# A message-passing layer: the tail's first one-hots stand two steps later in the written order

## The chip, the core and the metric

The kernel runs on one core of a Trainium2 chip. Its engines work side by side, each through its own list of instructions in order: PE multiplies matrices (its weight loads show as PEld), DVE and ACT work on vectors, POOL issues the scatters, SP issues most transfers. The time is device microseconds of one execution. Before the change three runs took 1111.35, 1112.56 and 1113.34 us; the median is 1112.56.

## What is computed

A graph layer with 6250 nodes, 100000 edges and 128 features:

```python
msg_in = jnp.concatenate([x[row], x[col], edge_attr], axis=-1)
h = msg_in @ W + b
mu = jnp.mean(h, axis=-1, keepdims=True)
var = jnp.mean(jnp.square(h - mu), axis=-1, keepdims=True)
h = (h - mu) * jax.lax.rsqrt(var + LN_EPS) * gamma + beta
out = jax.ops.segment_sum(jax.nn.relu(h), row, num_segments=x.shape[0])
...
x = _layernorm(x + out, axis=-1)
```

`row` is the source node of an edge, `col` its destination; the edges come sorted by destination.

## The kernel before

**Two halves that overlap.** The first half goes through the edges in pieces of four tiles of 128. For each piece PE multiplies edge features by a third of the weights and adds the destination's part (`edges`), ACT copies the result out of PSUM (`evict`), and POOL writes each row to its place in a DRAM table, sorted by source block (`scatters`, line 651, one indirect transfer for each tile). The edges are cut into seven splits, each with a table of its own (`sorted0` to `sorted6`). The second half reads the tables back, two source blocks (a "pair") at a time, and for each pair does this, with the engine in brackets:

- `load` (SP): the pair's rows into `hl`
- `ones` (DVE): `ohe`, one-hots of each row's node within its block
- `turn` (PE), `turned` (ACT): `ohe` transposed into `tr` and copied to `ohn`
- `seed` (ACT or PE) and `pick` (PE): the rows into a PSUM tile `sel` or `hp`, plus the source node's part by a product with `ohn`
- `square` (ACT): sums of squares, and their roots `std`
- `root`, `scale` (DVE): `rstd`, and the normalized, cut message `msg`
- `sums` (PE), `add` (DVE): messages summed by node into `pa`, and added to `acc`

**What sets the order.** PE, DVE, ACT and SP take instructions in the order in which the Python calls stand (`manual_schedule`). For the first six splits that order is made by `work(n)`: it takes n steps, and in each the table `FLOW` says which stage of which pair is issued. A pair starts every four steps. A pair with a single group of tiles is at `turn` two steps after its `ones`, at `turned` and `seed` after three, at `pick` after 5, `square` 7, `root` and `scale` 9, `sums` 10 and `add` 13. So several old pairs are in flight at any step.

**The tail.** The seventh split's pairs are done by `Unit` objects, U0 to U13 here, of one or two pairs each, with the same stages and a layer norm of the finished nodes at their end (`begin`, `stats`, `var`, `norm`, `end`). Their first load reads `sorted6` and so needs the last scatter to have landed. Between `work` and the loop over `tail(i)` there is a seam written out by hand, in which the last steps of the old pairs and the first stages of U0 and U1 alternate. The last old pair, the one before it and the one before that are called X, Y and W in this text. The seam starts at step `n_tail`, which is X's step 4, and ends after X's step 14, with its `add` at 13.

Names in the profile: an old pair's stages have the lines 749 (`ones`), 761 and 765 (`turn`, `turned`), 771 (`seed`), 788 (`pick`), 797 and 800 (`square`), 806, 812 (`root`, `scale`), 821 (`sums`), 827 (`add`); a unit's have 848 (`load`), 855, 865, 868, 875 (seed on ACT) or 877 (seed on PE), 888, 899 and 902, 907, 914, 928, 934. There are four `hl` buffers, so U3's load takes the place of X's rows and U4's that of U0's.

Of the kernel before, what the change touches and what calls it, by code (L numbers as in the profile page):

```python
# [85 lines left out]
def fast_path(ctx, tc, io, bad_d, found):  # L86
# [634 lines left out]
    def load_pairs(s, p, n):  # L721

        k = 2 * SPLITS[s][1]
        rows = late["blk"].tile([P, KMAX, ROW], F32, name="hl", bufs=4)
        for i in range(n):
            nc.sync.dma_start(flat(rows[:, i * k:(i + 1) * k, :]),
                              dram_ap(sorted_d[s], (p + i) * k * P * ROW,
                                      [[k * ROW, P], [1, k * ROW]]))
        loaded[s, p] = rows
# [362 lines left out]
    n_steps = 0  # L1092
# [28 lines left out]
    def work(n):  # L1121

        nonlocal n_steps
        for _ in range(n):
            for off, step in FLOW:
                i = n_steps - LEAD - off
                if i % 4 or not 0 <= i // 4 < len(pairs):
                    continue
                if step is None:
                    load_pairs(*pairs[i // 4])  # L1130
                    continue
                if off == 0:
                    at_work[i // 4] = Pairs(i // 4, *pairs[i // 4])
                step(at_work[i // 4])
            n_steps += 1
# [114 lines left out]
    n_tail = 4 * (len(pairs) - 1) + LEAD + 4  # L1250
    work(n_tail - n_steps)
    for i in range(3):
        units[i].load()
    work(1)
    units[0].ones()
    units[3].load()
    work(1)
# [6 lines left out]
    work(2)  # L1264
    units[1].turn()
    units[0].square()
    work(5)
    assert not steps_at and not others and all(cleared[s] == NB // 2 for s in cleared)
    units[2].ones()
    units[4].load()  # L1270
# [36 lines left out]
@with_exitstack  # L1307
def gnn_resnorm_kernel(ctx, tc, io):
    nc = tc.nc
    keep = ctx.enter_context(tc.tile_pool(name="keep", bufs=1))  # L1310
    bad_t = keep.tile([1, 1], I32, name="bad_t")
    with ExitStack() as inner:
        found = []
        fast_path(inner, tc, io, bad_t, found)
    with tc.If(found[0] > 0, preferred_fallthrough_block=True, label="general"):
        with ExitStack() as inner:
            general_path(inner, tc, io)
# [233 lines left out]
```

## Time and profile before

| | |
|---|---|
| median of three runs | 1112.56 us |
| the profiled execution | 1110.36 us |
| its span, first to last instruction | 1108.6 us |
| PE busy | 865.3 us (78%) |
| DVE busy | 858.5 us (77%) |
| ACT busy | 767.3 us (69%) |
| POOL busy | 796.4 us (72%) |
| last scatter on POOL | 1017.30, 0.87 long |
| U0's load issued on SP | 1019.44 |

Times within the span are us from its start. A row of the timeline has the start, the duration, the engine, the line, the operation with its output and inputs, how many instructions are merged in it, and in brackets how long the engine was idle before it and what ended that wait. Matmuls are pipelined, so rows of PE overlap. The granted clock is the share of full speed that TensorE had. Shares of the whole span say little here, since the change touches some 20 us near the end.

### The profile page before, as it was taken

How to read it: one execution, taken by the hardware profiler on the slowest of the kernel's cores; microseconds unless marked ns; L12 is line 12 of the kernel's file. 1: busy time of each engine (PE TensorE's matmuls, PEld its weight loads, DVE VectorE, ACT ScalarE, POOL GpSimd, SP SyncE). 2: the span in 40 equal slices, each digit the busy share in tenths (PEclk: the TensorE clock that was granted, in tenths of full speed). 3: DMA queues.
4: the chain of work that ended last, by engine and by line, in shares of the span. 5: the costliest groups of instructions: out<-in, count | busy, mean ns of one | idle time of the engine just before them, and what ended most of it. 6: DMA issues, size and time to landing. Idle time of an engine off the chain costs nothing. (4 is left out here: it accounts for less than half of the span.)

```text
span 1108.6 us, 27458 instructions
## 1 busy us (share of the span) xinstructions
PE 865.3 (78%) x8878; PEld 799.1 (72%) x8878; DVE 858.5 (77%) x2436; ACT 767.3 (69%) x3049; POOL 796.4 (72%) x830
## 2 busy tenths in 40 slices
PE   6758656456989898698868868788889788885994
PEld 4647545446889788688768868678888788875773
DVE  8874656636898997869687777889898977764997
ACT  4324422126889888588676778798889787976896
POOL 2777777777777777777777777777777777775254
PEclk9878887668999999889899989999999999998998
DMA  6899999648877888777587767686789777833341
GB/s 212 246 279 270 278 316 296 217 161 273 285 249 233 256 250 261 240 222 226 165 263 235 250 196 237 210 291 204 223 250 292 239 215 210 245 115 117 117 132 64
DMA packets 132851, 250.59 MB, mean 226 GB/s; under 512 B 47805, under 2 KB 62031, under 8 KB 132697
## 3 DMA queue, kind: packets, MB, share of 16 engines
q1 hardware_dynamic: 106724, 195.30, 59.0%
q0 software_dynamic: 25104, 53.05, 13.4%
q8 instruction: 71, 1.16, 0.5%
q14 instruction: 82, 0.67, 0.2%
q10 hardware_dynamic: 870, 0.40, 0.1%
HBM read 155.49 MB, written 93.18 MB: 224 GB/s over the span
## 5 line engine op out<-in xcount | busy, mean ns | idle before, releaser
L651 POOL DMA_INDIRECT sorted<-hs,place_i x782 | 758.1, 969 | 243.3 <-issue 96.6
L821 PE MATMUL pa<-msg,ohe 128*128 128x130 f32 x1700 | 237.1, 288 | 30.8 <-DVE acc L827 22.8
L788 PE MATMUL sel<-xa,ohn 128*128 128x128 bf16 x2550 | 190.9, 224 | 83.2 <-ACT sel L771 82.5
L620 PEld LDWEIGHTS hp<-w,eT 128*128 128x128 f32 x1564 | 216.7, 213 | 49.8 <-issue 29.2
L620 PE MATMUL hp<-w,eT 128*128 128x128 f32 x1564 | 238.5, 301 | 16.7 <-ACT hs L634 16.7
L797 ACT ACTIVATE sq<-sel 128x128 f32<-128x128 f32 x850 | 224.0, 279 | 39.2 <-PE sel L788 37.7
L812 DVE SCALAR_TENSOR_TENSOR msg<-sel,rstd,cut 128x128 f32<-128x128 f32 x850 | 243.0, 345 | 8.8
L821 PEld LDWEIGHTS pa<-msg,ohe 128*128 128x128 f32 x1700 | 211.0, 197 | 38.9 <-DVE acc L827 26.2
L788 PEld LDWEIGHTS <-ohn 128*128 128x128 bf16 x2550 | 165.0, 100 | 93.8 <-issue 85.4
L797 ACT ACTIVATION_READ_ACCUMULATOR sq<-sel 128x1 f32 x850 | 178.8, 210 | 0.0
L749 DVE TENSOR_TENSOR ohe<-hl,beside 128x768 f32<-128x768 f32 (+2 forms) x130 | 132.2, 1017 | 36.8 <-PE beside L503 21.3
L634 ACT COPY hs<-hp 128x512 f32<-128x512 f32 x196 | 113.1, 579 | 50.3 <-PE hp L624 47.6
L771 ACT COPY sel<-hl 128x384 f32<-128x384 f32 (+1 forms) x250 | 132.1, 529 | 19.9 <-DVE msg L812 19.2
L765 ACT COPY ohn<-tr 128x768 bf16<-128x768 bf16 (+2 forms) x130 | 109.6, 843 | 5.9 <-PE tr L761 5.9
L608 DVE TENSOR_SCALAR ohd<-db,part_w 128x512 bf16<-128x512 bf16 x192 | 69.6, 363 | 56.5 <-DMA db<-drel_d 31.0
L827 DVE TENSOR_TENSOR acc<-acc,pa 128x260 f32<-128x260 f32 x150 | 62.8, 419 | 51.9 <-PE pa L821 51.6
L569 ACT COPY hs<-sloc 128x12 f32<-128x12 f32 x66 | 14.1, 214 | 112.6 <-DMA sorted<-hs,place_i 110.8
L624 PE MATMUL hp<-win,ohd 126*128 126x128 bf16 x782 | 81.7, 230 | 1.7 <-DMA win<-xb_d 1.7
L761 PE MATMUL tr<-ident_h,ohe 128*128 128x128 bf16 x850 | 70.8, 223 | 13.3 <-issue 10.4
L800 ACT ACTIVATE std<-ss,eps 128x3 f32<-128x3 f32 (+1 forms) x250 | 74.2, 297 | 8.1
L806 DVE RECIPROCAL rstd<-std 128x3 f32<-128x3 f32 (+1 forms) x250 | 42.3, 169 | 46.7 <-ACT std L800 44.5
L624 PEld LDWEIGHTS <-ohd 126*128 126x128 bf16 x782 | 65.8, 104 | 5.4 <-issue 2.0
(200 smaller groups left out, 1033.0 us busy)
## 6 DMA issues: line engine op xcount, KB each, us to landing
eT<-in_eT SPq DMA_DIRECT2D x96, 512.0 KB
hl<-sorted SPq DMA_DIRECT2D x75, 396.0 KB
db<-drel_d SPq DMA_DIRECT2D x96, 256.0 KB
sorted<-empty SPq DMA_DIRECT2D x100, 198.0 KB
hl<-sorted SPq DMA_DIRECT2D x75, 264.0 KB
hl<-sorted SPq DMA_DIRECT2D x25, 528.0 KB
sorted<-hs,place_i POOLq DMA_INDIRECT x782
sorted<-empty SPq DMA_DIRECT2D x75, 132.0 KB
```

The costliest lines, as they stand in the source:

```text
L620: pe(nc.tensor.matmul(hp[:, j, :], eT[:, at], w[:, 2, :], start=j == 0, stop=False, skip_group_check=True), 4)
L624: pe(nc.tensor.matmul(hp[:, j, :], oh[:3 * WN, at], win[:3 * WN, :], start=False, stop=j == m - 1, skip_group_check=True))
L634: nc.scalar.copy(hs[:, :m, 0:D], hp[:, :m, :])
L651: i = nc.gpsimd.indirect_dma_start(out=sorted_d[s][:, :], out_offset=bass.IndirectOffsetOnAxis(ap=place_i[:parts, t:t + 1], axis=0), in_=h ...
L749: nc.vector.tensor_tensor(self.ohe[:, :k, :], self.hl[:, :k, D:D + 1].to_broadcast([P, k, P]), row_bc(iota_p, k), op=ALU.is_equal)
L765: nc.scalar.copy(self.ohn[:, :self.k, :], self.tr[:, :self.k, :])
L771: nc.scalar.copy(self.sel[g][:, :m, :], self.hl[:, j0:j0 + m, 0:D])
L788: pe(nc.tensor.matmul(sel[:, j, :], self.ohn[:, j0 + j, :], xa[:, b, i * D:(i + 1) * D], start=False, stop=j == m - 1 and i == 2, skip_gro ...
L797: nc.scalar.activation(sq[:, j, :], self.sel[g][:, j, :], AF.Square, accum_out=ss[:, j:j + 1])
L800: nc.scalar.activation(std[:, :m], ss[:, :m], AF.Sqrt, bias=eps, scale=1.0 / D)
L812: nc.vector.scalar_tensor_tensor(self.msg[:, j0 + j, 0:D], self.sel[g][:, j, :], rstd[:, j:j + 1], cut, op0=ALU.mult, op1=ALU.max)
L821: pe(nc.tensor.matmul(self.pa[:, h, :], self.ohe[:, i * k + j, :], self.msg[:, i * k + j, :], start=(j == h), stop=(j == k - 2 + h)), 4)
```

## The change

Two numbers in the seam. Before, one step of `work` stood ahead of U0's `ones` and five ahead of U2's; now it is three, and as many as make the same total. The number of instructions stays the same, and the orders on POOL and SP too.

```diff
     work(n_tail - n_steps)
     for i in range(3):
         units[i].load()
-    work(1)
+    work(3)
     units[0].ones()
     units[3].load()
     work(1)
@@
     work(2)
     units[1].turn()
     units[0].square()
-    work(5)
+    work(n_tail + 11 - n_steps)
```

On DVE, from W's `scale` on (`msg_2204` is Y's message, `msg_2205` that of W and then X; `ohe<-hl` at L855 is U0's `ones` and then U1's):

```order
 L812 SCALAR_TENSOR_TENSOR msg_2205<-sel,rstd,cut 128x128 x4
+L827 TENSOR_TENSOR acc<-acc,pa 128x260
+L806 RECIPROCAL rstd<-std 128x4
+L812 SCALAR_TENSOR_TENSOR msg_2204<-sel,rstd,cut 128x128 x4
 L855 TENSOR_TENSOR ohe<-hl,beside 128x512
 L827 TENSOR_TENSOR acc<-acc,pa 128x260
 L806 RECIPROCAL rstd<-std 128x4
-L812 SCALAR_TENSOR_TENSOR msg_2204<-sel,rstd,cut 128x128 x4
+L812 SCALAR_TENSOR_TENSOR msg_2205<-sel,rstd,cut 128x128 x4
 L855 TENSOR_TENSOR ohe<-hl,beside 128x1024
```

W's `add` and Y's `root` and `scale` moved ahead of U0's `ones`; Y's `add` and X's `root` and `scale` now stand between U0's and U1's `ones`.

On ACT, from Y's `square` on (`ohn<-tr` is U0's `turned`, `sel<-hl` its `seed`):

```order
 L797 ACTIVATE sq,ss<-sel 128x128 x4
 L800 ACTIVATE std<-ss,eps 128x4
+L797 ACTIVATE sq,ss<-sel 128x128 x4
+L800 ACTIVATE std<-ss,eps 128x4
 L868 COPY ohn<-tr 128x512
-L797 ACTIVATE sq,ss<-sel 128x128 x4
-L800 ACTIVATE std<-ss,eps 128x4
 L875 COPY sel<-hl 128x512
```

X's `square` moved ahead of U0's `turned`, so that U0's `seed` comes right behind it.

On PE, Y's `sums` moved ahead of U0's `turn` in the same way, and X's `sums` (`pa<-msg_2205`) ahead of U1's `turn` (`tr<-ident_h,ohe`), whose eight transposes stood between it and U0's `pick` (`sel<-xa,ohn`); the end of that `pick`:

```order
+L888 LDWEIGHTS ohn
+L888 MATMUL sel<-xa,ohn 128x128
+L821 MATMUL pa<-msg_2205,ohe 128x130 x4
 L865 LDWEIGHTS ohe
 L865 MATMUL tr<-ident_h,ohe 128x128
```

X's `sums` now follow U0's `pick` at once, and U1's transposes follow them.

## The prediction

> **What bounds the kernel now.** The edit touches only the seam between the old pairs and the tail, so after the page's first line I read the busy time of each engine by stage, then who waits for whom at the seam. In the stage rows the columns are the stretch, its length, the busy time of PE, PEld, DVE, ACT and POOL with their instruction counts, the granted TensorE clock, the DMA share and GB/s.
>
> ```profile
> span 1108.6 us, 27458 instructions
> ...
> 1015.00:1022.00 7.00, 0.28 (x6) 0.11 (x2) 0.00 (x0) 0.00 (x0) 2.56 (x3) 0.67 0.30 96
> 1022.00:1030.00 8.00, 6.56 (x43) 5.24 (x44) 6.02 (x16) 4.85 (x22) 0.00 (x0) 0.65 0.74 251
> 1030.00:1038.00 8.00, 7.43 (x91) 6.61 (x92) 7.21 (x19) 7.05 (x38) 0.68 (x1) 1.00 0.43 135
> 1038.00:1090.00 52.00, 51.16 (x490) 39.47 (x490) 50.70 (x211) 49.60 (x258) 29.52 (x28) 1.00 0.32 102
> ```
>
> From 1015 to 1022 PE, DVE and ACT stand still. From 1038 to 1090 DVE is busy 50.70 of 52 us: there every microsecond that DVE starts earlier is worth a microsecond at the end. Between these lies the ramp, 1022 to 1038, in which no engine is full. What the stall waits for is in the waits of 1000 to 1045 (us in total, times, longest), of the engines and then of SP's queue:
>
> ```profile
> DVE ohe L855 <- DMA hl<-sorted: 8.7, 2, 8.2
> ACT ohn L868 <- PE tr L865: 8.5, 1, 8.5
> ```
>
> ```profile
> SPq L848 <- DMA sorted<-hs,place_i: 17.1, 1, 17.1
> SPq L848 <- ACT sel L875: 4.7, 3, 3.1
> ```
>
> The tail's first load waits on SP for the last scatter. DVE waits 8.2 us in U0's one-hots for that load, and ACT, whose next instruction is U0's `turned`, waits 8.5 us behind it. Neither SP's nor POOL's order is changed, so the load lands at the same moment; the edit can only change what is left to do when it lands. I call the last three old pairs W, Y and X (X last).
>
> **What is left behind the wait.** DVE in order of time (start, us, instruction, and in brackets the idle time before it):
>
> ```profile
> 1022.11 0.69 DVE L855 TENSOR_TENSOR ohe<-hl,beside 128x512 f32<-128x512 f32 x1 [8.23 <-DMA hl<-sorted]
> 1022.72 0.42 DVE L827 TENSOR_TENSOR acc<-acc,pa 128x260 f32<-128x260 f32 x1
> 1023.05 0.17 DVE L806 RECIPROCAL rstd<-std 128x4 f32<-128x4 f32 x1
> 1023.25 1.13 DVE L812 SCALAR_TENSOR_TENSOR msg<-sel,rstd,cut 128x128 f32<-128x128 f32 x4
> ...
> 1024.88 1.22 DVE L855 TENSOR_TENSOR ohe<-hl,beside 128x1024 f32<-128x1024 f32 x1 [0.49 <-DMA hl<-sorted]
> ...
> 1028.99 0.43 DVE L827 TENSOR_TENSOR acc<-acc,pa 128x260 f32<-128x260 f32 x1 [1.31 <-PE pa L821]
> ...
> 1030.67 1.13 DVE L914 SCALAR_TENSOR_TENSOR msg<-sel,rstd,cut 128x128 f32<-128x128 f32 x4
> ...
> 1038.13 0.43 DVE L934 TENSOR_TENSOR acc<-acc,pa 128x260 f32<-128x260 f32 x1 [0.47 <-PE pa L928]
> ```
>
> ACT and PE at the same place:
>
> ```profile
> 1014.66 0.30 ACT L800 ACTIVATE std<-ss,eps 128x4 f32<-128x4 f32 x1
> 1023.50 0.58 ACT L868 COPY ohn<-tr 128x512 bf16<-128x512 bf16 x1 [8.55 <-PE tr L865]
> 1023.98 0.28 ACT L797 ACTIVATE sq<-sel 128x128 f32<-128x128 f32 x1
> ...
> 1025.36 0.58 ACT L875 COPY sel<-hl 128x512 f32<-128x512 f32 x1
> 1027.53 0.28 ACT L899 ACTIVATE sq<-sel 128x128 f32<-128x128 f32 x1 [1.59 <-PE sel L888]
> ...
> 1028.91 0.99 ACT L868 COPY ohn<-tr 128x1024 bf16<-128x1024 bf16 x1
> ...
> 1030.84 0.28 ACT L899 ACTIVATE sq<-sel 128x128 f32<-128x128 f32 x1 [0.45 <-PE sel L888]
> ```
>
> ```profile
> 1013.25 1.36 PE L821 MATMUL pa<-msg,ohe 128*128 128x130 f32 x8 [0.81 <-DVE msg L812]
> 1014.45 0.83 PE L788 MATMUL sel<-xa,ohn 128*128 128x128 bf16 x12
> 1022.86 0.61 PE L865 MATMUL tr<-ident_h,ohe 128*128 128x128 bf16 x4 [7.57 <-DVE ohe L855]
> 1023.75 2.09 PE L821 MATMUL pa<-msg,ohe 128*128 128x130 f32 x8 [0.29 <-DVE msg L812]
> 1025.99 1.44 PE L888 MATMUL sel<-xa,ohn 128*128 128x128 bf16 x12
> 1027.23 0.77 PE L865 MATMUL tr<-ident_h,ohe 128*128 128x128 bf16 x8
> 1027.84 1.11 PE L821 MATMUL pa<-msg,ohe 128*128 128x130 f32 x8
> 1028.79 1.02 PE L877 MATMUL sel<-hl,ident 128*128 128x512 f32 x2
> 1029.95 1.51 PE L888 MATMUL sel<-xa,ohn 128*128 128x128 bf16 x24
> 1031.30 0.61 PE L865 MATMUL tr<-ident_h,ohe 128*128 128x128 bf16 x8
> ```
>
> The chain through the ramp is: U0's `turned` (ACT 1023.50), X's squares (1023.98), U0's seed (1025.36), U0's `pick` (PE 1025.99), U0's squares (1027.53), U1's `turned` (1028.91), U1's `pick` (1029.95), U1's squares (1030.84), and so on through ACT and PE until DVE's last wait for PE at 1038.13, behind which DVE is full.
>
> **The change part by part.** (a) DVE: the add of W and the root and scale of Y go ahead of U0's one-hots. W's sums end at 1014.61 (1013.25 and 1.36) and Y's std at 1014.96, so they run at about 1015 to 1016.3, inside the 8.23 us of idle; 0.42 + 0.17 + 1.13 = 1.72 us of DVE work leaves the ramp. What stood behind them on DVE gains less, since U1's one-hots still wait for their load at 1024.88.
>
> (b) PE: Y's sums, 2.09 us at 1023.75, go ahead of U0's transposes and run at about 1016.3 in the stall. (c) ACT: X's squares and std go ahead of U0's `turned`. X's `pick` ends at 1015.28, so they too run in the stall. U0's seed then stands right behind `turned`, at 1023.98 instead of 1025.36: 1.38 us gained. The seed takes 0.58, PE starts 0.05 after its end (1025.94 to 1025.99), so U0's `pick` runs 1024.61 to 1026.05, and U0's squares, which start 0.10 after it and hold ACT 1.38 us (1027.53 to 1028.91), run 1026.15 to 1027.53.
>
> (d) PE: X's sums now stand between U0's `pick` and U1's transposes; before they stood behind the transposes. Here most of the 1.38 us is given back. They follow the `pick` as the transposes did, 1.24 us after its start (1025.99 to 1027.23): at 1025.85. Their msg is ready at 1024.38, since X's scale takes the place of Y's at 1023.25. Their price hangs on the clock: 2.09 us for the same eight matmuls at 1023.75, 1.11 at 1027.84. The clock's slots around the seam and two elsewhere (stretch, length, PE busy, clock, DMA share, GB/s):
>
> ```profile
> 1020.70:1024.10 3.40, 0.96 (x5) 0.50 0.95 301
> 1024.12:1027.52 3.40, 3.25 (x23) 0.50 0.78 278
> ...
> 146.90:150.30 3.40, 3.11 (x15) 0.50 1.03 335
> 150.33:153.73 3.40, 2.51 (x23) 1.00 1.00 302
> 532.60:536.00 3.40, 2.38 (x16) 0.50 0.50 141
> 536.03:539.40 3.37, 3.37 (x25) 0.50 0.46 143
> ```
>
> PE wakes at half clock and has the full clock from 1027.5 (the stage row from 1030 shows 1.00). If that stays, 1.65 us of X's sums run at half clock, 0.79 of them, and the rest takes 0.21 x 1.11 = 0.23: to 1027.74. U1's transposes (0.61 at full clock, 1031.30) end at about 1028.3, and U1's `turned` starts at 1028.31 instead of 1028.91: 0.60 gained. If X's sums stay at half clock throughout they end at 1027.94, and the transposes take between 0.77 (the row at 1027.23, half of it at half clock) and 1.22 (twice 0.61); with 1.0 in the middle `turned` starts at 1028.9: nothing gained there. U1's `pick` follows `turned` by 1.04 (1028.91 to 1029.95) and ACT and PE pass what is gained on until 1038. DVE can follow: it no longer waits 1.31 at 1028.99 with U2's one-hots behind the add, and reaches U0's scale about 1.1 us before 1030.67.
>
> (e) SP: U3's load keeps its place and what it waits for (X's seed, long done). U4's load waits for U0's seed, as the row of SP's waits on ACT shows, and goes out 1.38 us earlier; its data is wanted after 1035, so this is worth nothing. POOL's first order after the scatters is a `begin` behind DVE's adds and moves with them.
>
> Sum: bounds 1.38 gained (PE never late) and, with a slow clock, 0.9 lost (below); I take 0.5, near the 0.60 that this trace's own clock gives and a little under it, because part of the clock's positions give 0.3 to 0.5. The profiled execution took 1110.36 us with a span of 1108.6; that gives 1109.86. The median of the runs shown, 1112.56, is 2.20 above the profiled execution, so 1112.06, rounded 1112.0.
>
> **The page that speaks against it.** In the slot rows a half-clock slot with 3.25 of 3.40 us busy (0.96) or 3.11 (0.91) is followed by the full clock, one with 2.38 (0.70) by half clock again. After the change PE is busy in the slot 1024.12 to 1027.52 only from 1024.61: 0.86, between these rows. The Trainium skill, "TensorE: Matmul & The Clock Gate", section "What's actually happening", says that the full clock comes after a busy window of about 3.4 us and that the window is free-running. By that rule a PE that starts its dense work later can miss a window and pay one more. The trace agrees so far: the half clock ends at 1027.5 although PE woke at 1022.86.
>
> **The rivals.**
> A, slower: the clock returns one slot later, at 1030.94. Then X's sums and U1's transposes run at half clock, `turned` is at 1028.9, the seed matmuls of U1 (1.02 at 1028.79) take up to 2.04 and end at 1030.9, and the first 12 of U1's `pick` take 0.83 from there; U1's squares start at about 1031.75 instead of 1030.84: 0.9 lost, 1113.5. It decides where PE's dense work starts too late in a slot, 1024.61 instead of 1023.75. If a second slot is missed too (to 1034.4), U1's other 12 cost 0.6 more, and U1's sums, U2's seed and `pick` about 0.9 and 0.9: over 3 us lost, 1115.7. Against the second: from 1024.61 PE has no gap, so the next slot is full. Where the seam falls in a slot the edit does not set, and the two starts are 0.86 us apart in a slot of 3.41: in three positions of four both programs miss or catch the same one.
> B, full gain: 1.38 us, 1111.2, if X's sums do not hold up the transposes. For it: in the stretch before the stall the same sums cost 1.36 at full clock; against it, PE stands idle from about 1017.7, 5 us, and in this trace the clock fell within 2.0 us of the last matmul at 1015.28.
> C, hidden anyway: 1112.6. The ramp follows landings, not instructions. For it, U1's one-hots wait for their load at 1024.88 before and after; against it, U1's `turned` waits for ACT, not for that load.
>
> **How the numbers follow.** About 0.2%, 2.2 us, is what a measurement of this kernel can tell from no change. Chances: forecast (0.3 to 0.7 gained) 0.55, B 0.15, C 0.12, A with one slot 0.10, with two 0.08. The runs shown lie from 1.2 below their median to 0.8 above. Half of B and a tenth of the forecast may so come out over 2.2 faster: 0.13. A with two slots, a fifth of A with one and a little of C come out over 2.2 slower: 0.11. The rest, 0.76, is within. Range: from B less 1.0 of spread, 1110.2, to A with one slot, rounded 1113.6.
>
> **What would show it.** Right: DVE's add, reciprocal and scale (L827, L806, L812) before the long wait at L855; the squares L797 right behind X's `pick` near 1015.3; U0's seed L875 within 0.5 us of `turned`; eight L821 matmuls of about 2 us before U1's transposes; U1's `turned` about 6.2 us after U0's one-hots (now 6.80). Wrong: the stall itself shorter or longer than 8.2 us, or the half clock lasting past 8 us after U0's one-hots (now 5.4). Wrong in kind: DVE not full from 1038 on.

## The result, and the profile after

The changed kernel took 1112.56 us (median of 14 runs, 1110.88 to 1114.07), the kernel before 1113.01 (14 runs beside them, 1111.35 to 1114.04): a ratio of 0.9996, 95% interval 0.9988 to 1.0004. In the totals that is no change. What the edit did is seen only in the trace, counted from one event: R, the start of U0's one-hots (the first L855 on DVE), which comes 4.81 us after the last scatter starts before and 4.84 after.

The stages of the changed kernel, moved by 0.6 us with its last scatter (columns as in the prediction):

```profile
1015.60:1022.60 7.00, 1.62 (x13) 1.12 (x10) 1.26 (x6) 1.44 (x9) 2.54 (x3) 0.90 0.30 96
1022.60:1030.60 8.00, 5.76 (x47) 4.77 (x48) 5.66 (x14) 4.02 (x13) 0.00 (x0) 0.66 0.73 251
```

The stall is no longer empty: PE is busy 1.62 us in it instead of 0.28, DVE 1.26 and ACT 1.44 instead of nothing, and each has less to do in the ramp. DVE in order of time:

```profile
1015.22 0.43 DVE L827 TENSOR_TENSOR acc<-acc,pa 128x260 f32<-128x260 f32 x1 [0.77 <-PE pa L821]
1015.56 0.17 DVE L806 RECIPROCAL rstd<-std 128x4 f32<-128x4 f32 x1
1015.77 1.13 DVE L812 SCALAR_TENSOR_TENSOR msg<-sel,rstd,cut 128x128 f32<-128x128 f32 x4
1022.73 0.69 DVE L855 TENSOR_TENSOR ohe<-hl,beside 128x512 f32<-128x512 f32 x1 [5.83 <-DMA hl<-sorted]
...
1028.37 0.43 DVE L827 TENSOR_TENSOR acc<-acc,pa 128x260 f32<-128x260 f32 x1 [1.86 <-PE pa L821]
1028.71 1.21 DVE L855 TENSOR_TENSOR ohe<-hl,beside 128x1024 f32<-128x1024 f32 x1
```

W's add and Y's root and scale stand ahead of the long wait, which shrank from 8.23 to 5.83 us, and R (1022.73) did not move against the scatter. ACT and PE:

```profile
1015.89 0.28 ACT L797 ACTIVATE sq<-sel 128x128 f32<-128x128 f32 x1 [0.37 <-PE sel L788]
...
1024.12 0.58 ACT L868 COPY ohn<-tr 128x512 bf16<-128x512 bf16 x1 [6.76 <-PE tr L865]
1024.61 0.60 ACT L875 COPY sel<-hl 128x512 f32<-128x512 f32 x1
...
1028.82 1.01 ACT L868 COPY ohn<-tr 128x1024 bf16<-128x1024 bf16 x1 [0.56 <-PE tr L865]
```

```profile
1016.27 1.36 PE L821 MATMUL pa<-msg,ohe 128*128 128x130 f32 x8 [0.41 <-DVE msg L812]
1023.48 0.61 PE L865 MATMUL tr<-ident_h,ohe 128*128 128x128 bf16 x4 [5.85 <-DVE ohe L855]
1025.25 1.44 PE L888 MATMUL sel<-xa,ohn 128*128 128x128 bf16 x12 [1.17 <-ACT sel L875]
1026.48 1.85 PE L821 MATMUL pa<-msg,ohe 128*128 128x130 f32 x8
1028.17 0.61 PE L865 MATMUL tr<-ident_h,ohe 128*128 128x128 bf16 x8
```

U0's seed comes 0.49 us after its `turned`, U0's `pick` at R+2.52 (before R+3.88). Then X's sums take 1.85 us on PE, ACT waits 0.56 us for U1's transposes, and U1's `turned` starts at R+6.09 (before 6.80). The chains of the two kernels, before and then after, end with the same row:

```profile
1102.63 0.34 DVE y L982
```

```profile
1102.56 0.34 DVE y L982
```

From R to the end of that row it is 80.86 us before (1102.63 + 0.34 - 1022.11) and 80.17 after: 0.69 gained. Each value is of one execution; how well such a value repeats is seen below in `act_alone` and `act_alone_2`, the same kernel twice: 80.42 and 80.37. The span is longer all the same (1109.1 against 1108.6), since in this execution the last scatter came 0.59 us later and 6.2 instead of 5.6 us followed the last DVE row. No instruction that the edit moved lies in either place.

### The profile page after: what moved, and what is told of

Read it like the earlier page. It is cut to its first block, busy times and chain, and to the rows that moved or that the text cites. A ratio compares the mean times of both kernels' runs of the same rounds, so it can differ in the third digit from the quotient of the medians.

```text
span 1109.1 us, 27457 instructions
## 1 busy us (share of the span) xinstructions
PE 869.6 (78%) x8878; PEld 803.4 (72%) x8878; DVE 859.7 (78%) x2436; ACT 767.5 (69%) x3049; POOL 796.0 (72%) x830
## 5 line engine op out<-in xcount | busy, mean ns | idle before, releaser
L821 PE MATMUL pa<-msg,ohe 128*128 128x130 f32 x1700 | 241.6, 291 | 31.1 <-DVE acc L827 23.9
L821 PEld LDWEIGHTS pa<-msg,ohe 128*128 128x128 f32 x1700 | 215.0, 200 | 39.3 <-DVE acc L827 27.3
L749 DVE TENSOR_TENSOR ohe<-hl,beside 128x768 f32<-128x768 f32 (+2 forms) x130 | 132.0, 1016 | 33.5 <-PE beside L503 20.8
```

The source lines that it names most:

```text
L749: nc.vector.tensor_tensor(self.ohe[:, :k, :], self.hl[:, :k, D:D + 1].to_broadcast([P, k, P]), row_bc(iota_p, k), op=ALU.is_equal)
L821: pe(nc.tensor.matmul(self.pa[:, h, :], self.ohe[:, i * k + j, :], self.msg[:, i * k + j, :], start=(j == h), stop=(j == k - 2 + h)), 4)
```

## The experiments

The runs went to several chips. The two profiles above and the run `all_first_2` are from chips on which the kernel before takes 1111 to 1113 us. The others fell on two chips on which the same kernel takes 1354.4 us (median of 35 runs) and 1352.3 (29). There the seam is another one, as the first experiment shows, and I say for each what it still tells. The kernel before was profiled only where there is a stall. All times are counted from R; "end" is the end of the last DVE row.

| | U0's `pick` | U1's `turned` | U1's squares | end | clock around the ramp |
|---|---|---|---|---|---|
| before | 3.88 | 6.80 | 8.73 | 80.86 | half from -4.79 to 5.45 |
| after | 2.52 | 6.09 | 8.03 | 80.17 | half from -1.56 to 5.27 |
| all_first_2 | 2.52 | 5.43 | 7.36 | 79.51 | half from -1.43 to 5.40 |
| after_again | 2.30 | 4.60 | 6.53 | 78.65 | full |
| act_alone | 4.01 | 6.32 | 8.25 | 80.42 | full |
| act_alone_2 | 4.01 | 6.31 | 8.24 | 80.37 | full |
| act_kept | 3.66 | 7.57 | 9.51 | 81.68 | half from 3.76 to 7.17 |
| pe_kept | 2.98 | 6.74 | 8.69 | 80.84 | half from 0.62 to 4.03 |
| sums_behind | 2.30 | 4.60 | 6.85 | 79.00 | full |
| sums_behind_2 | 2.30 | 4.60 | 8.52 | 80.65 | half from 4.43 to 7.84 |
| all_first | 2.51 | 5.42 | 7.58 | 79.72 | half from 0.16 to 6.99 |
| after_warm | 6.95 | 9.25 | 11.18 | 83.30 | full |
| all_first_warm | 3.60 | 5.91 | 7.84 | 79.98 | full |
| warm_2 | 4.03 | 6.33 | 8.26 | 80.39 | half from -3.05 to 0.36 |

The first three rows are from the chips with a stall, the others from those without. Without a stall R itself moves with the old DVE work that stands ahead of it, so there only runs with the same DVE order ahead of U0's one-hots can be compared by R: `after_again`, `act_kept`, `pe_kept`, the two `sums_behind` and `after_warm`. The runs `act_alone`, `act_kept`, `pe_kept` and `sums_behind` were timed once each, 1354.73, 1356.64, 1355.68 and 1356.08 us with 1353.43 for before beside them; on chips where runs of one kernel lie some 20 us apart, these totals tell nothing.

**The changed kernel once more.**

> The changed kernel once more, for another position of the clock's slots. Theory: the full clock returns between R+5.0 and R+8.5 by the position; with a return by R+5.5 U1's turned is at R+6.1 and the end at R+80.2, with a return at R+8.5 U1's turned at R+6.8 and the end at up to R+81.3. Rival (the return follows a fixed time after the first matmul): R+5.3 again and the same end to 0.1 us.

Measured: 1354.1 us against 1354.41, ratio 0.9991 (0.9965 to 1.0017). Both expectations missed, since the half clock never came. On this chip the old pairs are late and there is no stall. DVE ahead of U0's one-hots (L749 is X's), and PE behind them:

```profile
1263.65 0.68 DVE L749 TENSOR_TENSOR ohe<-hl,beside 128x512 f32<-128x512 f32 x1
...
1266.95 0.42 DVE L827 TENSOR_TENSOR acc<-acc,pa 128x260 f32<-128x260 f32 x1 [0.77 <-PE pa L821]
1267.91 0.18 DVE L806 RECIPROCAL rstd<-std 128x4 f32<-128x4 f32 x1 [0.53 <-ACT std L800]
1268.12 1.12 DVE L812 SCALAR_TENSOR_TENSOR msg<-sel,rstd,cut 128x128 f32<-128x128 f32 x4
1269.16 0.67 DVE L855 TENSOR_TENSOR ohe<-hl,beside 128x512 f32<-128x512 f32 x1
```

```profile
1271.46 0.83 PE L888 MATMUL sel<-xa,ohn 128*128 128x128 bf16 x12 [1.17 <-ACT sel L875]
1272.13 1.11 PE L821 MATMUL pa<-msg,ohe 128*128 128x130 f32 x8
1273.08 0.61 PE L865 MATMUL tr<-ident_h,ohe 128*128 128x128 bf16 x8
```

L855 has no wait before it: R is set by the old work on DVE, 11.37 us after the last scatter starts, not by the load. And PE, kept busy, has the full clock: U0's `pick` takes 0.83 instead of 1.44, X's sums 1.11 instead of 1.85. The end is then R+78.65, 1.52 us sooner than the same order at half clock (80.17). So this run, meant for the position of the clock's slots, shows about what the half clock costs the ramp. That the missing stall makes little of the difference, the same order with and without one shows: in `all_first_2` and `all_first` below, both at half clock, U1's `turned` comes at R+5.43 and 5.42.

**One part kept back at a time.** First X's squares stay between U0's `turned` and `seed`:

```diff
-    work(1)
     units[0].turn()
-    work(1)
     units[0].turned()
-    work(1)
+    work(2)
+    work(1)
     units[0].pick(0, nc.scalar)
```

> PE and DVE in the changed order, but X's squares stay between U0's turned and U0's seed as before. Theory: the seed and so U0's pick stay at R+3.88, and X's sums now stand between that pick and U1's transposes: U1's turned at R+6.9 to 7.8, end R+80.9 to 81.8, no gain or up to 1 us lost against before. Rival (the gain comes from the 1.72 us that leave DVE): U1's turned before R+6.8, end about R+80.2 as after the change.

U1's `turned` came at R+7.57 and the end at R+81.68, within the theory's ranges but with some luck: there is no stall here, and the half clock that the theory counts on came only as one slot from R+3.76. U0's `pick` waits for the seed, and X's sums at half clock then stand in front of U1's transposes:

```profile
1270.80 1.38 PE L888 MATMUL sel<-xa,ohn 128*128 128x128 bf16 x12 [2.53 <-ACT sel L875]
1271.98 2.04 PE L821 MATMUL pa<-msg,ohe 128*128 128x130 f32 x8
```

What does not hang on that slot is the `pick`: R+3.66 against 2.30 in `after_again`, which has the same orders on DVE and PE. The rival, that the work taken off DVE is the gain, does not fit this: DVE has the changed order here, and 1.36 us are lost at the `pick`. How much of it would reach the end at full clock was not seen; X's sums alone took 2.04 us here and 1.11 in `after_again`. Then Y's sums stay behind U0's transposes:

```diff
-    work(3)
+    work(2)
     units[0].ones()
     units[3].load()
-    work(1)
     units[0].turn()
-    work(1)
+    work(2)
     units[0].turned()
-    work(1)
+    work(2)
     units[0].pick(0, nc.scalar)
```

> DVE and ACT in the changed order, but Y's sums stay behind U0's transposes on PE as before. Theory: Y's sums start at R+1.4 at half clock, 2.09 us, so U0's pick starts at about R+3.5; X's sums follow it, and U1's turned is at R+7.0 to 7.4, end R+81.0 to 81.4: 0.2 to 0.5 us slower than before. Rival (PE's part is hidden): as after the change, U1's turned R+6.1, end R+80.2.

End R+80.84, 2.19 later than the changed order on the same kind of chip (`after_again`), a half clock from R+0.62 to 4.03 being part of it: at this clock PE's part is not hidden. Y's sums also reach U1 by way of DVE, which the theory left out. Y's add waits for them, U1's one-hots stand behind that add, and U1's transposes wait for these one-hots (DVE, then PE):

```profile
1270.24 0.43 DVE L827 TENSOR_TENSOR acc<-acc,pa 128x260 f32<-128x260 f32 x1 [2.54 <-PE pa L821]
```

```profile
1273.10 0.62 PE L865 MATMUL tr<-ident_h,ohe 128*128 128x128 bf16 x8 [0.45 <-DVE ohe L855]
```

The end was 0.2 us better than the theory's band, because Y's sums started at R+1.1, behind the transposes at once, and the half clock ended at R+4.03. Then the squares alone, in the old order:

```diff
     units[0].turn()
-    work(1)
-    units[0].turned()
-    work(1)
+    work(2)
+    units[0].turned()
     units[0].pick(0, nc.scalar)
```

> Only X's squares go ahead of U0's turned; PE and DVE keep the order of before. Read from the start of U0's one-hots (R). Before: U0's pick R+3.88, U1's turned R+6.80, U1's squares R+8.73, last DVE instruction ends R+80.86; after the change 2.52, 6.09, 8.04, 80.17. Theory (the chain runs through ACT and PE in turn): Y's sums still stand ahead of U0's pick and end at R+3.73, so the pick starts at R+3.8 and at most 0.1 us is gained: U1's turned R+6.7, end R+80.75. Rival (ACT's 1.38 us is the gain by itself): pick R+2.5, U1's turned R+5.4, end R+79.5.

> Only X's squares ahead of U0's turned, PE and DVE as before, where the stall is there. Theory: U0's pick waits for Y's sums on PE, R+3.75 instead of 3.88, U1's turned R+6.7, end R+80.7, at most 0.15 us gained over before (80.87). Rival (ACT's 1.38 us is the gain by itself): pick R+2.5, U1's turned R+5.4 to 6.1, end R+79.5 to 80.2.

R+80.42 and R+80.37, nearer the theory's 80.7 than its rival, but for a reason of this chip: X's `pick` came late, its squares ran until 1268.96 in the first of the two runs, and held U0's `turned` back to R+2.90. The seed, not Y's sums, let the `pick` start at R+4.01. So whether the squares alone gain anything where there is a stall stays open. R also stands earlier here than in `after_again`, with less old work ahead of it. Counted from X's one-hots instead, which no edit moved, the end comes after 83.56 and 84.25 us, and after 84.17 in `after_again`: without a stall, these executions show no gain of the whole change over its squares alone. The timed ratio of the second run was 0.9993 (0.9963 to 1.0023).

**The price of X's sums in their new place.** They go behind U1's transposes:

```diff
     units[1].ones()
-    work(2)
     units[1].turn()
     units[0].square()
     work(n_tail + 11 - n_steps)
```

> The changed order, but X's sums go behind U1's transposes again. It measures what X's sums at that place cost. Theory: U1's turned then waits for ACT alone and comes at R+5.4 instead of 6.09, but PE has the same work ahead of U1's pick, X's sums at R+4.7 to 6.5 and U1's seed matmuls to R+7.4: U1's squares at R+8.2 against 8.04, end R+80.2 to 80.4, nothing gained over the change. Rival (the place of X's sums alone gives back 0.7 us): U1's squares R+7.4, end R+79.5.

> The changed order with X's sums behind U1's transposes, where the stall is there (R is the start of U0's one-hots, 4.8 us after the last scatter starts). Theory: U1's turned waits for ACT alone, R+5.4, but PE has X's sums and U1's seed matmuls ahead of U1's pick: U1's squares at R+7.9 to 8.3, end R+80.0 to 80.4, nothing gained over the change (80.17). Rival (the place of X's sums alone gives back 0.7 us): U1's squares R+7.4, end R+79.5.

At full clock (first run) U1's `turned` stays at R+4.60, but U1's squares come 0.32 later than with the changed order and the end 0.35 later. In the second run, half clock from R+4.43, the squares come at R+8.52. In both, the sums only change places with what U1's `pick` needs. At full clock this is what the theory says, nothing gained, and the place of X's sums is not what to mend. For the second run there is no changed order with the same half clock to set beside it. The second run's ratio was 1.0005 (0.9975 to 1.0034). Both runs had no stall, so the R+5.4 expected for `turned` at half clock was not seen.

**All old work first.**

```diff
-    work(3)
+    work(n_tail + 11 - n_steps)
     units[0].ones()
     units[3].load()
-    work(1)
     units[0].turn()
-    work(1)
     units[0].turned()
-    work(1)
     units[0].pick(0, nc.scalar)
     units[1].ones()
-    work(2)
     units[1].turn()
     units[0].square()
-    work(n_tail + 11 - n_steps)
```

> All old work ahead of U0's one-hots, once more, where the old pairs are done before the tail's first load lands (the runs before this one were on a chip on which the kernel of before takes 1353 us and DVE is still busy with old pairs when that load lands). R is the start of U0's one-hots. Theory: with the stall there, R does not move against the last scatter (R 4.8 us after the last scatter starts), U0's pick R+2.5, U1's turned R+5.4, U1's squares R+7.4 to 7.7, end R+79.5 to 79.8. Rival (the ramp is bound by landings): end R+80.2 as after the change. If the stall is missing here too, R comes 10 us or more after the last scatter and nothing is gained.

This run met the stall: R 4.78 us after the last scatter. 1109.30 us (8 runs, 1108.74 to 1111.07) against 1111.01 for before on the same chip (9 runs): ratio 0.9986, interval 0.9975 to 0.9997. DVE and PE:

```profile
1019.60 0.43 DVE L827 TENSOR_TENSOR acc<-acc,pa 128x260 f32<-128x260 f32 x1 [0.77 <-PE pa L821]
1022.12 0.69 DVE L855 TENSOR_TENSOR ohe<-hl,beside 128x512 f32<-128x512 f32 x1 [2.10 <-DMA hl<-sorted]
1023.80 1.22 DVE L855 TENSOR_TENSOR ohe<-hl,beside 128x1024 f32<-128x1024 f32 x1 [0.99 <-DMA hl<-sorted]
1025.59 1.22 DVE L855 TENSOR_TENSOR ohe<-hl,beside 128x1024 f32<-128x1024 f32 x1 [0.57 <-DMA hl<-sorted]
```

```profile
1018.20 1.36 PE L821 MATMUL pa<-msg,ohe 128*128 128x130 f32 x8 [1.08 <-DVE msg L812]
...
1024.64 1.44 PE L888 MATMUL sel<-xa,ohn 128*128 128x128 bf16 x12 [1.17 <-ACT sel L875]
1025.87 1.06 PE L865 MATMUL tr<-ident_h,ohe 128*128 128x128 bf16 x8
```

The last old add ends 2.10 us before the load lands, so X's sums, too, are paid in the stall. U1's `turned` is at R+5.43, the end at R+79.51: 1.35 us better than before and 0.66 better than the change, each within 0.1 us of what was expected. The totals, 1.71 apart with some 1.2 to each side, agree. The rival (landings bound the ramp) falls: U1's and U2's one-hots wait for their loads here, and U1's `turned` still came 0.66 sooner.

The same kernel on a chip without the stall:

> All that is left of the old pairs (also Y's add, X's root, scale, sums and add) stands ahead of U0's one-hots. Theory: it all fits in the stall of some 8 us, and PE has less ahead of U1's pick: U0's pick R+2.5, U1's turned R+5.4, U1's squares R+7.4 to 7.7, end R+79.5 to 79.8, that is 0.4 to 0.7 us better than the change (80.17) and 1.1 to 1.4 better than before (80.86); 0.10 to 0.12% of the whole. Rival (the landings of the loads bound the ramp): nothing more than the change, end R+80.2.

```profile
1254.99 0.68 DVE L749 TENSOR_TENSOR ohe<-hl,beside 128x512 f32<-128x512 f32 x1
...
1261.91 1.13 DVE L812 SCALAR_TENSOR_TENSOR msg<-sel,rstd,cut 128x128 f32<-128x128 f32 x4
1263.81 0.42 DVE L827 TENSOR_TENSOR acc<-acc,pa 128x260 f32<-128x260 f32 x1 [0.77 <-PE pa L821]
1264.15 2.94 DVE L855 TENSOR_TENSOR ohe<-hl,beside 128x512 f32<-128x512 f32 x3
```

1358.0 us, ratio 1.0030 (1.0000 to 1.0059), where 0.10% faster was expected. The one-hots of U0, U1 and U2 now stand behind all the old work with no wait for a load. The last scatter is no measure of what that costs: R comes 14.76 us after it here, while two runs with one and the same DVE order ahead of R, `after_again` and `sums_behind`, have 11.37 and 15.67. From X's one-hots, R comes after 9.16 us here (1264.15 - 1254.99) and after 5.51 in `after_again`: what is free in a stall is paid for here.

**Keeping PE at full clock.** Matmuls of no use, `hp<-ones_h`, are to fill the stall: 22 in the changed order, 12 with all old work first, and 12 with 4 more behind U0's transposes.

```diff
     work(3)
+    ps = psum.tile([P, PT, P], F32, name="hp", bufs=2)
+    for _ in range(22):
+        nc.tensor.matmul(flat(ps), ones_h, row_bc(ones_h, PT), start=True, stop=True)
     units[0].ones()
```

> The changed kernel with 22 matmuls of no use (128x512 bf16, 0.21 us each at full clock) on PE between Y's sums and U0's transposes, so that PE is busy through the stall. Theory (the half clock sets the price of X's sums and U0's pick): PE has the full clock at R, U0's pick takes 0.83, X's sums 1.1, U1's turned comes at R+4.9, U1's squares at R+6.8, end R+78.9 to 79.2, 1.7 to 1.9 us better than before. Rival (the waits are for ACT and the loads, the clock is of no account): as the change, end R+80.2. The matmuls can also end later than U0's one-hots and delay the transposes.

> Both: all old work ahead of U0's one-hots and 12 matmuls of no use behind it on PE. Theory: U0's pick R+2.5 at full clock, U1's turned R+4.85 (ACT's squares of U0), U1's squares R+6.8, end R+78.9, no better than with the full clock alone, since ACT is then the chain; 1.9 us better than before, 0.17%. Rival (the clock is of no account): as with all old work first, R+79.5 to 79.8.

> All old work ahead of U0's one-hots, and matmuls of no use (128x512 bf16) on PE: 12 behind X's sums and 4 behind U0's transposes, so that PE stays busy until U0's pick. Theory: PE has the full clock at U0's pick, so that takes 0.83 instead of 1.44 us; U1's turned R+4.6, U1's squares R+6.5, end R+78.6 to 78.8 against R+79.5 with all old work first; against before 2.0 to 2.2 us or 0.19% better. Rival (ACT and the landings bound the ramp whatever the clock): as with all old work first, R+79.5, 1.4 us better than before.

All three fell on chips without a stall and tell nothing of the theory: 1358.11 us (ratio 1.0019, 0.9989 to 1.0049), 1360.87 (1.0045, 1.0018 to 1.0072) and 1356.8 (1.0043, 1.0020 to 1.0066). PE had work enough, and the matmuls stood in its way; in the first, U0's transposes waited for them:

```profile
1267.92 4.91 PE L1257 MATMUL hp<-ones_h 128*128 128x512 bf16 x22
1272.67 0.39 PE L865 MATMUL tr<-ident_h,ohe 128*128 128x128 bf16 x4
```

Whether they would gain the 0.9 us that lie between R+79.51 and R+78.65 where there is a stall was not seen.

## Why the prediction was right, and where it was not

**The size.** 0.5 us was forecast, 0.60 for this trace's own clock; 0.69 was gained from R, and 0.45 lies between the medians, whose interval is about 0.9 us to each side. The total cannot tell the 0.5 from nothing, as the prediction said; R can. So it means little that the total lies within the range, which holds "no change" too. With 14 runs the least change that can be told was 0.9 us, not the 2.2 that I gave.

**(a) to (c)** came as worked out: the DVE work and Y's sums in the stall, X's squares right behind X's `pick` (expected near 1015.3, came at 1015.89 in an execution 0.6 later), U0's `pick` at R+2.52 for R+2.50.

**(d)** X's sums took 1.85 us for 1.88, and U1's `turned` came at R+6.09 for R+6.20, since the transposes ended 0.1 sooner than I let them. Both rest on the full clock coming back at R+5.27, near the R+5.45 of before. The forecast took this for the likely case but had no reason why the clock should come back just there: in part it was luck. That X's sums give back about half of the gain, all_first_2 bears out from the other side: with them, and what is left on DVE, out of the ramp and ACT's order the same, 0.66 more is gained.

One step of (d) was wrong. I wrote that DVE no longer waits for X's sums with U2's one-hots behind the add. In the changed kernel X's add still stands ahead of U2's one-hots, and DVE waits there longer than before, 1.86 us instead of 1.31 (rows 1028.37 and 1028.71 above). It cost nothing, since the sums end sooner: U2's one-hots start at R+5.98 instead of 7.22, and U0's scale (L914) at R+7.32 instead of 8.56, 1.24 sooner where I had 1.1.

**Rival A** did not come. The slot that I had put between the rows, at 0.86 busy, was even less busy, and the clock returned (slots of the changed kernel, columns as in the prediction):

```profile
1024.60:1028.00 3.40, 2.75 (x19) 0.50 1.01 361
1028.02:1031.42 3.40, 3.21 (x41) 1.00 0.15 41
```

2.75 of 3.40 is 0.81. As far as these rows tell, this was luck too. Elsewhere in the same trace a slot that was busier, 2.80 or 0.82, was followed by half clock again:

```profile
212.23:215.63 3.40, 2.80 (x14) 0.50 0.20 67
215.65:219.05 3.40, 3.40 (x17) 0.50 0.21 65
```

So the busy time of these rows does not decide near 0.8, and how close the changed kernel came to losing a slot stays open. That the positions vary where there is a stall was not seen: the clock returned at R+5.45, 5.27 and 5.40 in the three such runs. Without a stall it returned at R+4.03, 6.99, 7.17 and 7.84, at other places within a slot of 3.41 us. The Trainium skill, "TensorE: Matmul & The Clock Gate", section "What's actually happening", has the window free-running; the three runs are too few to speak against it, and the four agree with it.

**Rival B** named the right sum and the wrong way to it. In a stall 1.35 us came with X's sums out of the ramp (all_first_2), and not by the change alone. At full clock the changed ramp is shorter still (after_again), but what the edit gains there is not shown, since the kernel before has no profile at full clock.

**Rival C** falls with all_first_2.

**What the prediction did not see**: it took the stall for granted. On the chips without it the same edit moved nothing that can be measured (0.9991), and with more work moved forward the time was 0.30% longer, at the edge of its interval. I had no row for that, but what the edit is worth hangs on it, and it should have been a rival.

## What to carry to other kernels

Work that is ready can be put ahead of an instruction that waits for a transfer for nothing, but only as far as the wait lasts: compare the end of the moved work with the landing, on every engine that waits behind it, and ask what happens if the landing comes first. What stays behind the wait is paid at the price of the engine's state after it, here half a clock, so move whole chains (squares, root, scale, sums) rather than the one instruction next to the wait. A gain of half a microsecond in a millisecond is read from a fixed event in the trace, not from medians.

## What the runs showed of the hardware

The same kernel before took 1111 us on one chip and 1354 and 1352 on two others. The transfers themselves take as long: of SP's queue, the changed kernel on a quick chip and then on a slow one,

```profile
q1 hardware_dynamic: 106724, 195.30, 59.0%
```

```profile
q1 hardware_dynamic: 106724, 195.30, 48.9%
```

are 0.590 x 1109.1 = 654 us and 0.489 x 1354.1 = 662. So the 245 us more are not time of the packets. The slow chip's trace puts large ones down to no engine of this core, as in this row of its waits:

```profile
ACT hs L634 <- remote: 145.3, 36, 12.8
```

What makes them was not tried. Of the clock: a half clock that came alone lasted 3.41 us (R+3.76 to 7.17 in `act_kept`). In the changed kernel's trace a slot with PE busy 0.81 of it was followed by the full clock, and one with 0.82 was not.
